# A pre-norm block on one core: the high parts of the probabilities from PSUM, and a new order of issue

## The chip, the cores and the metric

The kernel runs on one core of a Trainium2 chip. The metric is the device time of one execution in microseconds, taken as the median of several runs; the profile shows one further execution with the hardware profiler on.

## The reference

The reference is one transformer block in fp32 over `x` of 4 x 2048 x 256: local attention with 16 heads of 16 elements and a causal window of 64 keys, and then an FFN with ternary weights. Both read a layer norm of their input and are added to it.

```python
q, k, v = proj(h, Wq), proj(h, Wk), proj(h, Wv)          # h = layernorm(x)
scores = einsum('bhqd,bhkd->bhqk', q, k) / 4 + bias       # bias: 0 where i-64 < j <= i, else -inf
x = x + einsum('bsd,ed->bse', softmax(scores) @ v, Wo)
W1q, W2q = quantize(W1), quantize(W2)                     # -1, 0, 1
x = x + relu(layernorm(x) @ W1q.T + b1) @ W2q.T + b2
```

## The kernel before

The 8192 rows are cut into 32 chunks of 256 rows, eight to a sequence. TensorE multiplies in fp16, and every fp32 operand is split into a high part (its rounding to fp16) and a low part (what is left), so that a product is two or three matmuls.

For one chunk the work is this. `load` and `norm_in` fetch the rows, normalize them and transpose them by DMA. `project` makes q, k and v (L635, L627) and their two parts. `stack` copies the parts of q and k by six DMAs (L692) into a buffer `st`, in which one slot per head holds queries, keys, and the keys once more shifted by 64; the shifted copy is made on DVE, the last 64 keys of the chunk before at L705 (at L703 zeros in the first chunk of a sequence) and the rest at L708. `maxima` multiplies queries and keys in 32-row tiles into a PSUM tile `sp` of which there is one (L731), DVE reduces it to the maximum of each row (L738), and four such steps make the maxima of a chunk. ACT scales them (L744), PE transposes them (L750), ACT copies them out (L753), and a DMA on SP's queue writes them as one more row into the stack (L756), so that the following product already has the maximum subtracted.

`weights` then runs eight times for a chunk, for four blocks of 64 queries and two groups of eight heads: eight matmuls of 64 columns (L771) fill one PSUM bank `tp`, ACT takes the exponential into an fp32 tile `pf` in SBUF (L781), ACT casts `pf` to its high part `ph` (L784), and POOL subtracts the two to the low part `pl` (L786). There is a second path with the low part on DVE, which the planner did not take once in this build. `values` multiplies both parts with v (L812 to L814) and divides by the sum (L827, L830). `wo_out` is the output projection (L850 transposes by DMA, L861, L865), the second norm (L573 on ACT with L569 and L570 on POOL, or L577 on DVE; casts and low parts at L579 and L583) and its transposition by DMA (L873). `ffn1` (L896, with L915 on ACT and L917 on DVE, or L906 to L911 with the low part on POOL) and `ffn2` (L936, L937, L942) end the chunk, and L945 stores it.

Six PSUM banks are shared by three kinds of tiles: `lin` (projections and FFN), `tp` (scores) and `pv` (values). A tile's bank is given back by `put`.

The order of the instructions is not that of the source. Each step is a Python generator that yields what it needs next: an engine (`"P"`, `"A"`, `"D"`, `"G"`, `"S"` for PE, ACT, DVE, POOL and SP) with an assumed duration, a buffer, or a signal. `Lanes.run` keeps a clock of its own for each engine and starts, of the steps that could start first, the one with the lowest priority number; the priorities come from the chunk's number and the tables `PRIO`, `SLOPE` and `EARLY` (the last for chunks 0, 1 and 2), less `BOOST` while a step holds a PSUM tile. `Lanes.pick` chooses between ways to do a step by the engines' loads so far, weighted by `WT`. `Lanes.chain` then fixes the order on each engine, SP included, so each engine issues its instructions strictly in the planned order.

```python
cost = [sum(t * math.exp((self.load[e] * WT[e] - top) / TAU) for e, t in o) for o in options]
lanes.add(c * (1 + SLOPE[kind]) + PRIO[kind] + early + 0.001 * k, gen)
```

Of the kernel before, what the change touches and what calls it, by code (L numbers as in the profile page):

```python
# [14 lines left out]
AF = mybir.ActivationFunctionType  # L15
# [4 lines left out]
D = 256  # L20
H = 16
HD = 16
W = 64
FF = 1024
EPS = 1e-5
C = 256
# [4 lines left out]
SW = 16.0  # L31
# [3 lines left out]
NQ = 3  # L35
NV = 3
PARTS = slice(64, 112)
R = 113
BIGH = 60000.0
PRIO = {'norm': 22.87, 'proj': 45.21, 'max': -15.41, 'att': 28.99, 'val': -103.79, 'wo': -72.86, 'ffn': -195.42, 'ffn2': 67.42, 'mask': 69.79, 'prep': -8.89}  # L40
SLOPE = {'norm': 0.0, 'proj': 0.051, 'max': 0.158, 'att': 0.043, 'val': 0.156, 'wo': 0.0, 'ffn': -0.016, 'ffn2': 0.0, 'mask': 0.106, 'prep': -0.017}
BUFS = {'xt': 11, 'ln': 2, 'xT': 3, 'zT': 4, 'qk': 2, 'pp': 6, 'op': 2, 'o': 2, 'h': 7, 'r': 5, 'bank': 6, 'lin': 6, 'sp': 1, 'tp': 3, 'pv': 4}
BANKS = ("lin", "tp", "pv")
EARLY = {'norm': (0.0, 0.0, -1.01), 'proj': (0.0, 6.69, -1.97), 'max': (0.0, 0.0, 0.0), 'att': (0.0, -2.82, 0.0), 'val': (0.0, 6.48, 0.0), 'wo': (0.0, 0.0, -1.66), 'ffn': (0.0, 0.0, 0.0), 'ffn2': (0.69, 0.0, -3.29), 'mask': (0.0, 0.0, 0.0), 'prep': (0.0, -20.19, 0.0)}
TOL = 0.0
BOOST = 4.14
CHAIN = ('PE', 'DVE', 'Activation', 'Pool', 'SP')
LAT = {"P": 0.2, "A": 0.17, "D": 0.15, "G": 0.13, "S": 0.97}
TAU = 17.1
DMAF, DLAT = 1.06, 0.78  # L50
WINDOW = 3.4133
WT = {'P': 0.82, 'A': 1.13, 'D': 1.02, 'G': 0.94, 'S': 0.0}


class Lanes:
# [21 lines left out]
    def put(self, pool):  # L77
        self.slots[pool].append(self.cur[0])
        self.wake(("get", pool))
        if pool == "sp":  # L80
            self.cur[1] += BOOST
        if pool in BANKS:
            self.cur[1] += BOOST
            self.slots["bank"].append(self.cur[0])
            for k in BANKS:
                self.wake(("get", k))
# [9 lines left out]
    def pick(self, options):  # L96

        top = max(self.load[e] * WT[e] for e in "PADG")
        cost = [sum(t * math.exp((self.load[e] * WT[e] - top) / TAU) for e, t in o) for o in options]
        return cost.index(min(cost))  # L100
# [47 lines left out]
    def run(self):  # L148
        while self.ready:
# [29 lines left out]
            if what == "get":  # L179
# [3 lines left out]
                if arg in BANKS or arg == "sp":  # L183
                    task[1] -= BOOST
            elif what == "S":
# [17 lines left out]
def kernel(ctx: ExitStack, tc: tile.TileContext, x, Wq, Wk, Wv, Wo, W1, b1, W2, b2, out):  # L203
    nc = tc.nc
    B, S, _ = x.shape
# [4 lines left out]
    lanes = Lanes(tc, BUFS)  # L210
# [25 lines left out]
    def get(name):  # L236
        return ("get", name)

    def wait(*key):
        return ("wait", key)  # L240

    def signal(*key):
        lanes.signal(key)
# [3 lines left out]
    def start(kind, c, gen, k=0):  # L247
        early = EARLY[kind][int(c)] if c < 3 else 0.0
        lanes.add(c * (1 + SLOPE[kind]) + PRIO[kind] + early + 0.001 * k, gen)

# [8 lines left out]
    st = [const.tile([128, 3, H, C], HP, name=f"st{i}") for i in range(NQ)]  # L259
# [25 lines left out]
    def constants():  # L285
        yield "G", 0.4
        make_identity(nc, ident)
        yield "D", 0.605
        nc.vector.memset(mhalf, -0.5)
        nc.vector.memset(ones, 1.0)  # L290
        nc.vector.memset(shift, PSHIFT * 4.0)
        signal("const")
        yield "D", 0.3
        nc.vector.tensor_copy(identh, ident)
        signal("ident")
        for i in range(NV):
            yield "G", 0.9
            nc.gpsimd.memset(vot[i][:, :, :, :, 32:34], 0.0)
            nc.gpsimd.memset(vot[i][:, 0, :, :, 32:33], 1.0)
            nc.gpsimd.memset(vet[i][0:64, :, 0], 0.0)  # L300
            nc.gpsimd.memset(mht[i % NQ], 0.0)
            signal("vfree", i - NV)
# [36 lines left out]
    def loaded(src, key):  # L339
        yield get("xt")  # L340
        yield "S", (0.5, 0.9)
        wn = xpool.tile([128, 2, D], FP, name="xt")
        nc.sync.dma_start(out=wn, in_=src)
        wts[key] = wn
        signal("loaded", key)
# [162 lines left out]
    def load(c):  # L508
        if c >= 2:
            yield wait("normed", c - 2)  # L510
        yield get("xt")
        yield "S", (0.55, 0.9)
        xt = xpool.tile([128, NT, D], FP, name="xt")
        nc.sync.dma_start(out=xt, in_=xf[c * C:(c + 1) * C, :].rearrange("(t p) d -> p t d", p=128))
        xts[c] = xt
        signal("x", c)
# [159 lines left out]
    def stack(c):  # L676
        first = c % NCB == 0
        yield wait("used", c - NQ)
        s = st[c % NQ]
        if first or (c >= NQ and (c - NQ) % NCB == 0):  # L680

            yield "S", (0.6, 0.1)
            nc.sync.dma_start(
                out=s[R - 1:R, 0], in_=(qone if first else qcon[R - 1:R]).unsqueeze(1).to_broadcast([1, H, C])
            )
            lanes.cur[0] = lanes.free["S"]

        for nm, g, parts in (("q", 0, "hhl"), ("k", 1, "hlh")):
            yield wait(nm, c)
            for n, part in enumerate(parts):  # L690
                yield "S", (0.68, 0.8)
                nc.sync.dma_start(  # L692
                    out=s[64 + n:112:3, g].rearrange("r h t -> r (h t)"),
                    in_=ps_["hl", c][:, g, "hl".index(part)].rearrange("p e t -> p (e t)"),
                )
                if g == 0 or n < 2:
                    lanes.cur[0] = lanes.free["S"]
        ps_.pop(("hl", c))
        put("qk")
        signal("stack", c)  # L700
        yield "D", 0.85
        if first:
            nc.vector.memset(s[PARTS, 2, :, 0:W], 0.0)  # L703
        else:
            nc.vector.tensor_copy(s[PARTS, 2, :, 0:W], st[(c - 1) % NQ][PARTS, 1, :, C - W:])  # L705
            used(c - 1)
        yield "D", 1.4
        nc.vector.tensor_copy(s[PARTS, 2, :, W:], s[PARTS, 1, :, 0:C - W])  # L708
        for b in range(NB):
            start("max", c, maxima(c, b), b)  # L710
            start("val", c, values(c, b), b)

    def place(j):
        return j % 8 * 2 + j // 8

    def window(c, h, b):
        return st[c % NQ][:, 1 if b % 2 else 2, h, b // 2 * 128:b // 2 * 128 + 128]

    def used(c):
        if tally(("used", c), 2 * NB + ((c + 1) % NCB > 0)):  # L720
            signal("used", c)

    def maxima(c, u):
# [35 lines left out]
        for b in range(NB):  # L759
            for g in range(2):  # L760
                start("att", c, weights(c, b, g), 2 * b + g)

    def weights(c, b, g):
        yield get("pp")
        yield get("tp")
        yield "P", 0.24
        tp = tps.tile([128, 8, W], FP, name="bank")
        for i in range(8):
            j = g * 8 + i
            h = place(j)  # L770
            nc.tensor.matmul(tp[:, i], window(c, h, b)[0:R + 1], st[c % NQ][0:R + 1, 0, h, b * W:b * W + W], start=True, stop=True)  # L771
        used(c)
        tpf = tp.rearrange("p h q -> p (h q)")
        ph = pp.tile([128, 4, 128], HP, name="ph")
        pl = pp.tile([128, 4, 128], HP, name="pl")
        phf, plf = (t.rearrange("p a b -> p (a b)") for t in (ph, pl))
        if lanes.pick([[("D", 0.605), ("A", 0.97)], [("G", 1.2), ("A", 1.005)]]):
            yield get("r")
            yield "A", 0.485
            pf = rp.tile([128, 512], FP, name="r")  # L780
            nc.scalar.activation(pf, tpf, AF.Exp, scale=0.25 / (SW * SW))  # L781
            put("tp")
            yield "A", 0.52
            nc.scalar.copy(phf, pf)  # L784
            yield "G", 1.2
            nc.gpsimd.tensor_tensor(plf, pf, phf, ALU.subtract)  # L786
            put("r")
        else:
            yield "A", 0.485
            nc.scalar.activation(tpf, tpf, AF.Exp, scale=0.25 / (SW * SW))  # L790
            yield "A", 0.485
            nc.scalar.copy(phf, tpf)
            yield "D", 0.605
            nc.vector.tensor_tensor(plf, tpf, phf, ALU.subtract)
            put("tp")
        ps_[c, b, g] = (ph, pl)
        signal("p", c, b, g)
# [148 lines left out]
        put("xt")  # L946

    for i, gen in enumerate([constants(), load(0)]):
        lanes.add(-9 + i, gen)
    for i, (nm, src) in enumerate((("q", Wq), ("k", Wk), ("v", Wv))):  # L950
        lanes.add(-7 + i, loaded(src.rearrange("(c p) d -> p c d", p=128), nm))
        start("proj", 0, weight_qkv(nm), i - 5)
    for c in range(NCH):
        if c:
# [34 lines left out]
```

## Time and profile before

| What | us |
|---|---|
| median of 3 runs (lowest, highest) | 670.91 (670.79, 671.71) |
| profiled execution | 671.55 |
| its span, first to last instruction | 669.8 |
| PE busy in the span | 626.2 |
| POOL, DVE, ACT busy | 558.5, 556.4, 529.1 |
| mean granted TensorE clock | 0.987 of full |

Busy time is the union of an engine's instructions; matmuls overlap one another, so a busy PE is not a PE at its peak. A line of a group reads: source line, engine, operation, output and input tiles, shapes, count, busy time in all, mean duration in ns, and the idle time of the engine just before with what ended it. A line of waits reads: who waited, for whom, us in total, how often, the longest. In the tables of stretches each engine has its busy time and, in brackets, its instructions; then come the granted clock, the DMA share and GB/s.

### The profile page before, as it was taken

The numbers are of one execution on the slowest core, as the hardware profiler recorded it, in microseconds if no ns is written. First come the engines' busy times: TensorE is split into PE (matmuls) and PEld (weight loads), VectorE is DVE, ScalarE is ACT, GpSimd is POOL, SyncE is SP. The second block draws the span as 40 slices with busy tenths as digits, with TensorE's granted clock in tenths as the row PEclk, the third lists the DMA queues.
The fourth block names the chain that finished last, engine by engine and source line by source line (L and its number), as shares of the span: only waits on it lengthen the run. The fifth ranks groups of instructions, "written<-read, shape, count | busy, mean of one in ns | idle before, by whom it ended". The sixth has DMA issues, their size and how long they took to land.

```text
span 669.8 us, 30496 instructions
## 1 busy us (share of the span) xinstructions
PE 626.2 (93%) x12892; PEld 548.3 (82%) x12892; DVE 556.4 (83%) x1195; ACT 529.1 (79%) x1074; POOL 558.5 (83%) x639
## 2 busy tenths in 40 slices
PE   2867889999999999999999999999999999999997
PEld 1646777888888888888888879898788888988986
DVE  6788989888987998898989898878878997897763
ACT  6966969877999689988879969686879589987741
POOL 5676989979899879998989979898789689998830
PEclk9977998999999999999999999999999999999999
DMA  6684465766777668865785665589555954542232
GB/s 180 167 154 107 82 130 115 120 129 109 138 132 127 133 115 132 146 115 142 143 140 127 131 96 141 119 142 145 90 124 126 156 122 106 116 107 60 49 81 62
DMA packets 165032, 81.34 MB, mean 121 GB/s; under 512 B 110880, under 2 KB 162848, under 8 KB 164896
## 3 DMA queue, kind: packets, MB, share of 16 engines
q1 hardware_dynamic: 164896, 79.39, 61.5%
q8 instruction: 101, 1.65, 1.2%
q14 instruction: 35, 0.29, 0.2%
HBM read 11.67 MB, written 8.39 MB: 30 GB/s over the span
## 4 chain that ended last, share of the span: by engine, by line
PE 56%; POOL 13%; DVE 11%; ACT 7%; DMA 6%; issue 5%; SPq 3%; POOLq 0%; DVEq 0%; ACTq 0%
PE bank L896 11%; PE bank L635 7%; POOL pl L786 7%; PE bank L771 6%; PE bank L936 6%; PE bank L937 5%; PE sp L731 5%; PE bank L861 5%; PE bank L627 3%; DMA xt<-in_dram 3%; PE bank L814 3%; PE bank L812 2%; PE bank L813 2%; DVE mx L738 2%; ACT ph L784 2%
## 5 line engine op out<-in xcount | busy, mean ns | idle before, releaser
L786 POOL TENSOR_TENSOR pl<-r,ph 128x512 f16<-128x512 f32 x256 | 304.5, 1210 | 17.3 <-ACT ph L784 10.9
L781 ACT ACTIVATE r<-bank 128x512 f32<-128x512 f32 x256 | 145.5, 599 | 32.2 <-PE bank L771 26.9
L784 ACT CAST ph<-r 128x512 f16<-128x512 f32 x256 | 151.0, 629 | 0.7
L738 DVE TENSOR_REDUCE mx<-sp 128x8 f32<-128x768 f32 x128 | 121.8, 952 | 14.7 <-PE sp L731 13.0
L896 PE MATMUL bank<-zT,wq 128*128 128x256 f16 x1024 | 125.5, 273 | 0.3 <-DVE hl L917 0.2
L936 PE MATMUL bank<-wq,hh 128*128 128x256 f16 x512 | 119.7, 273 | 0.0
L937 PE MATMUL bank<-wq,hl 128*128 128x256 f16 x512 | 119.2, 272 | 0.0
L917 DVE SCALAR_TENSOR_TENSOR hl<-bank,hh 128x512 f16<-128x512 f32 x126 | 85.2, 685 | 34.8 <-ACT hh L915 33.2
L896 PEld LDWEIGHTS <-wq 128*128 128x128 f16 x1024 | 97.8, 98 | 12.5 <-issue 0.3
L915 ACT ACTIVATE hh<-bank 128x512 f16<-128x512 f32 x126 | 75.4, 604 | 31.9 <-PE bank L896 31.7
L771 PE MATMUL bank<-st 114*128 114x64 f16 x2048 | 86.9, 194 | 3.8 <-DMA st<-mst 1.4
L812 PEld LDWEIGHTS <-ph 128*128 128x128 f16 x1024 | 82.3, 96 | 4.2 <-DVE o L830 1.8
L814 PEld LDWEIGHTS <-pl 128*128 128x128 f16 x1024 | 79.9, 96 | 5.0 <-POOL pl L786 4.4
L771 PEld LDWEIGHTS <-st 114*128 114x128 f16 x2048 | 74.5, 98 | 11.4 <-issue 2.8
L813 PEld LDWEIGHTS <-ph 128*128 128x128 f16 x1024 | 80.5, 96 | 1.8 <-issue 0.6
L830 DVE TENSOR_TENSOR o<-bank,rec 64x128 f32<-64x128 f32 x256 | 73.8, 288 | 8.4 <-POOL nb L570 0.5
L731 PE MATMUL sp<-st 113*32 113x96 f16 x4096 | 69.7, 211 | 9.5 <-DVE mx L738 4.8
L731 PEld LDWEIGHTS <-st 113*32 113x32 f16 x4096 | 51.3, 98 | 26.9 <-issue 23.9
L936 PEld LDWEIGHTS <-hh 128*128 128x128 f16 x512 | 49.8, 97 | 6.0
L937 PEld LDWEIGHTS <-hl 128*128 128x128 f16 x512 | 50.0, 98 | 4.7
L597 POOL TENSOR_TENSOR op<-o,op 128x512 f16<-128x512 f32 x32 | 39.2, 1225 | 16.6 <-ACT op L844 16.0
L526 DVE BATCH_NORM_STATS2 st<-xt 128x6 f32<-128x256 f32 x128 | 47.8, 415 | 6.0 <-DMA xt<-in_dram 5.0
(117 smaller groups left out, 1493.0 us busy)
## 6 DMA issues: line engine op xcount, KB each, us to landing
st<-hl SPq DMA_DIRECT2D x192, 128.0 KB, 4.1
xt<-in_dram SPq DMA_DIRECT2D x44, 256.0 KB, 4.1
out_dram<-xt SPq DMA_DIRECT2D x32, 256.0 KB, 2.7
ve<-vo SPq DMA_DIRECT2D x32, 136.0 KB, 2.6
ve<-vo SPq DMA_DIRECT2D x60, 68.0 KB, 3.3
oT<-op SPq DMA_TRANSPOSE x64, 3.2
xT<-ht SPq DMA_TRANSPOSE x32, 3.5
st<-mst SPq DMA_DIRECT2D x32, 8.0 KB, 2.2
```

The costliest lines, as they stand in the source:

```text
L731: nc.tensor.matmul(sp[32 * n:32 * n + 32, p, 0:96], st[c % NQ][0:R, 0, h, b * W + q * 32:b * W + q * 32 + 32], window(c, h, b)[0:R, 32 * q ...
L738: nc.vector.tensor_reduce(ps_["mx", c][:, u], sp[:, :, 0:96], AX.X, ALU.max)
L771: nc.tensor.matmul(tp[:, i], window(c, h, b)[0:R + 1], st[c % NQ][0:R + 1, 0, h, b * W:b * W + W], start=True, stop=True)
L781: nc.scalar.activation(pf, tpf, AF.Exp, scale=0.25 / (SW * SW))
L784: nc.scalar.copy(phf, pf)
L786: nc.gpsimd.tensor_tensor(plf, pf, phf, ALU.subtract)
L812: nc.tensor.matmul(pv[:, p, :], ph[:, i, :], v[:, 0, b // 2, p, :], start=True, stop=False)
L813: nc.tensor.matmul(pv[:, p, 0:32], ph[:, i, :], v[:, 1, b // 2, p, 0:32], start=False, stop=False)
L814: nc.tensor.matmul(pv[:, p, :], pl[:, i, :], v[:, 0, b // 2, p, :], start=False, stop=True)
L896: nc.tensor.matmul(ps[:, u], wq1[:, d + d * i, fs], zT[:, i, d], start=n == 0, stop=n == 3)
L936: nc.tensor.matmul(ps[:, t, :], hh[:, f % 2, ts], wq2[:, f, :], start=f == 0, stop=False)
L937: nc.tensor.matmul(ps[:, t, :], hl[:, f % 2, ts], wq2[:, f, :], start=False, stop=f == NF - 1)
```

## The change

There are three edits. In `weights`, on the path that is taken, the high part is no longer cast from `pf` in SBUF: ACT takes the exponential of the same PSUM tile a second time, with fp16 as its output, and the bank is given back after that (`put("tp")` stands one instruction later). In `stack`, the copy of the last 64 keys may go to ACT or DVE by `Lanes.pick`, and the booked durations of the two copies change. The planner's tables change in some entries, so that the order of issue on every engine is another one. `FIRST` is 0 and changes nothing.

```diff
-PRIO = {'norm': 22.87, 'proj': 45.21, 'max': -15.41, 'att': 28.99, ...}
-SLOPE = {'norm': 0.0, ..., 'mask': 0.106, 'prep': -0.017}
+PRIO = {'norm': 22.87, 'proj': 45.21, 'max': -15.28, 'att': 28.41, ...}
+SLOPE = {'norm': 0.051, ..., 'mask': 0.069, 'prep': -0.017}
-EARLY = {..., 'att': (0.0, -2.82, 0.0), 'val': (0.0, 6.48, 0.0), 'wo': (0.0, 0.0, -1.66), ...}
+EARLY = {..., 'att': (4.07, -2.82, 0.0), 'val': (0.0, 6.48, 0.0), 'wo': (0.0, -3.23, -1.66), ...}
-BOOST = 4.14
+FIRST = 0.0
+BOOST = 3.75
-WT = {'P': 0.82, 'A': 1.13, 'D': 1.02, 'G': 0.94, 'S': 0.0}
+WT = {'P': 0.82, 'A': 1.13, 'D': 1.02, 'G': 0.9, 'S': 0.0}
...
-        yield "D", 0.85
         if first:
+            yield "D", 0.85
             nc.vector.memset(s[PARTS, 2, :, 0:W], 0.0)
         else:
-            nc.vector.tensor_copy(s[PARTS, 2, :, 0:W], st[(c - 1) % NQ][PARTS, 1, :, C - W:])
+            old = (s[PARTS, 2, :, 0:W], st[(c - 1) % NQ][PARTS, 1, :, C - W:])
+            if lanes.pick([[("D", 0.7)], [("A", 0.95)]]):
+                yield "A", 0.95
+                nc.scalar.copy(*old)
+            else:
+                yield "D", 0.7
+                nc.vector.tensor_copy(*old)
             used(c - 1)
-        yield "D", 1.4
+        yield "D", 1.5
         nc.vector.tensor_copy(s[PARTS, 2, :, W:], s[PARTS, 1, :, 0:C - W])
...
-        if lanes.pick([[("D", 0.605), ("A", 0.97)], [("G", 1.2), ("A", 1.005)]]):
+        if lanes.pick([[("D", 0.605), ("A", 0.97)], [("G", 1.2), ("A", 0.97)]]):
             yield get("r")
             yield "A", 0.485
             pf = rp.tile([128, 512], FP, name="r")
             nc.scalar.activation(pf, tpf, AF.Exp, scale=0.25 / (SW * SW))
+            yield "A", 0.485
+            nc.scalar.activation(phf, tpf, AF.Exp, scale=0.25 / (SW * SW))
             put("tp")
-            yield "A", 0.52
-            nc.scalar.copy(phf, pf)
             yield "G", 1.2
             nc.gpsimd.tensor_tensor(plf, pf, phf, ALU.subtract)
             put("r")
...
-        lanes.add(-9 + i, gen)
+        lanes.add(FIRST - 9 + i, gen)
```

More of the change, by code (lines that the diff above doesn't have):

```diff
@@ L39 @@
 BIGH = 60000.0
-PRIO = {'norm': 22.87, 'proj': 45.21, 'max': -15.41, 'att': 28.99, 'val': -103.79, 'wo': -72.86, 'ffn': -195.42, 'ffn2': 67.42, 'mask': 69.79, 'prep': -8.89}
-SLOPE = {'norm': 0.0, 'proj': 0.051, 'max': 0.158, 'att': 0.043, 'val': 0.156, 'wo': 0.0, 'ffn': -0.016, 'ffn2': 0.0, 'mask': 0.106, 'prep': -0.017}
+PRIO = {'norm': 22.87, 'proj': 45.21, 'max': -15.28, 'att': 28.41, 'val': -103.79, 'wo': -72.86, 'ffn': -195.42, 'ffn2': 67.42, 'mask': 69.79, 'prep': -8.89}
+SLOPE = {'norm': 0.051, 'proj': 0.051, 'max': 0.158, 'att': 0.043, 'val': 0.156, 'wo': 0.0, 'ffn': -0.016, 'ffn2': 0.0, 'mask': 0.069, 'prep': -0.017}
 BUFS = {'xt': 11, 'ln': 2, 'xT': 3, 'zT': 4, 'qk': 2, 'pp': 6, 'op': 2, 'o': 2, 'h': 7, 'r': 5, 'bank': 6, 'lin': 6, 'sp': 1, 'tp': 3, 'pv': 4}
 BANKS = ("lin", "tp", "pv")
-EARLY = {'norm': (0.0, 0.0, -1.01), 'proj': (0.0, 6.69, -1.97), 'max': (0.0, 0.0, 0.0), 'att': (0.0, -2.82, 0.0), 'val': (0.0, 6.48, 0.0), 'wo': (0.0, 0.0, -1.66), 'ffn': (0.0, 0.0, 0.0), 'ffn2': (0.69, 0.0, -3.29), 'mask': (0.0, 0.0, 0.0), 'prep': (0.0, -20.19, 0.0)}
+EARLY = {'norm': (0.0, 0.0, -1.01), 'proj': (0.0, 6.69, -1.97), 'max': (0.0, 0.0, 0.0), 'att': (4.07, -2.82, 0.0), 'val': (0.0, 6.48, 0.0), 'wo': (0.0, -3.23, -1.66), 'ffn': (0.0, 0.0, 0.0), 'ffn2': (0.69, 0.0, -3.29), 'mask': (0.0, 0.0, 0.0), 'prep': (0.0, -20.19, 0.0)}
 TOL = 0.0
-BOOST = 4.14
+FIRST = 0.0
+BOOST = 3.75
 CHAIN = ('PE', 'DVE', 'Activation', 'Pool', 'SP')
@@ L948 @@
     for i, gen in enumerate([constants(), load(0)]):
-        lanes.add(-9 + i, gen)
+        lanes.add(FIRST - 9 + i, gen)
     for i, (nm, src) in enumerate((("q", Wq), ("k", Wk), ("v", Wv))):
-        lanes.add(-7 + i, loaded(src.rearrange("(c p) d -> p c d", p=128), nm))
+        lanes.add(FIRST - 7 + i, loaded(src.rearrange("(c p) d -> p c d", p=128), nm))
         start("proj", 0, weight_qkv(nm), i - 5)
```

## The prediction

> **What bounds the kernel now.** I read the page's busy shares first, then the chain, then a table of five stretches, because a mean over 670 us hides that the first 66 us are another regime.
>
> ```profile
> PE 626.2 (93%) x12892; PEld 548.3 (82%) x12892; DVE 556.4 (83%) x1195; ACT 529.1 (79%) x1074; POOL 558.5 (83%) x639
> PE 56%; POOL 13%; DVE 11%; ACT 7%; DMA 6%; issue 5%; SPq 3%; POOLq 0%; DVEq 0%; ACTq 0%
> 0.00:66.00 66.00, 39.14 (x531) 29.94 (x532) 50.54 (x114) 48.18 (x102) 42.37 (x63) 0.90 0.68 154
> 66.00:100.00 34.00, 29.00 (x801) 25.64 (x798) 30.01 (x66) 28.25 (x60) 30.58 (x31) 1.00 0.54 102
> 100.00:130.00 30.00, 28.62 (x606) 24.68 (x602) 25.94 (x59) 26.98 (x56) 28.89 (x37) 0.94 0.71 122
> 130.00:660.00 530.00, 523.58 (x10918) 463.07 (x10916) 447.70 (x956) 425.06 (x858) 456.65 (x511) 1.00 0.63 120
> 660.00:670.00 10.00, 5.86 (x54) 5.00 (x52) 2.21 (x4) 0.60 (x1) 0.00 (x0) 1.00 0.15 52
> ```
>
> In the stretches the columns are length, then busy time of PE, weight load, DVE, ACT and POOL, then the granted clock. PE is the bound: from 130 to 660 us it idles 530 - 523.58 = 6.4 us. It idles 26.9 us before 66 us, 5.0 from 66 to 100, 1.4 from 100 to 130 and 4.1 in the last ten. PE does the same matmuls after the change, so its work stays; only idle and slow-clock time can move. In the order of issue, PE's two programs are alike until the transpose of the second chunk's maxima (66 us in this trace), and the last rows are the same final FFN matmuls. So the 26.9 us and the 4.1 us stay, and what can be won is 5.0 + 1.4 + 6.4 = 12.8 us of idle and one slow-clock stretch:
>
> ```profile
> 104.60:108.01 3.41, 2.04 (x83) 1.83 (x79) 3.27 (x11) 3.41 (x8) 3.35 (x5) 1.00 0.44 72
> 108.01:111.42 3.41, 3.41 (x43) 2.63 (x39) 2.57 (x5) 2.44 (x7) 3.33 (x5) 0.50 0.32 60
> ```
>
> Half clock for 3.41 us costs 1.7 us. What PE and the queues wait for (total us, times, longest):
>
> ```profile
> PE sp L731 <- DVE mx L738: 4.8, 7, 1.4
> PE bank L814 <- POOL pl L786: 3.3, 4, 1.2
> PE bank L771 <- DMA st<-mst: 1.4, 1, 1.4
> PE bank L812 <- DVE o L830: 1.4, 1, 1.4
> PE bank L771 <- DVE hl L917: 1.3, 1, 1.3
> POOL pl L786 <- ACT ph L784: 10.9, 8, 3.4
> SPq L850 <- POOL pl L786: 27.4, 13, 4.5
> ```
>
> These are single events, not a pattern.
>
> **The change part by part.** The sum is made against the profiled execution, 671.55 us (span 669.8 and 1.75 around it); the median of the runs, 670.91, lies 0.64 lower.
>
> *Second exponential.* 256 casts from SBUF become 256 exponentials from PSUM.
>
> ```profile
> L786 POOL TENSOR_TENSOR pl<-r,ph 128x512 f16<-128x512 f32 x256 | 304.5, 1210 | 17.3 <-ACT ph L784 10.9
> L781 ACT ACTIVATE r<-bank 128x512 f32<-128x512 f32 x256 | 145.5, 599 | 32.2 <-PE bank L771 26.9
> L784 ACT CAST ph<-r 128x512 f16<-128x512 f32 x256 | 151.0, 629 | 0.7
> L915 ACT ACTIVATE hh<-bank 128x512 f16<-128x512 f32 x126 | 75.4, 604 | 31.9 <-PE bank L896 31.7
> ```
>
> No row is an exponential from PSUM to f16; the nearest are the same exponential to f32 (599 ns) and a relu from PSUM to f16 (604 ns). So ACT saves 256 x (629 - 604) = 6.4 us, at most 256 x (629 - 599) = 7.7. ACT is 79% busy and off the path nearly everywhere: the chain gives L784 2%, 13.4 us, of which 25/629 is 0.5 us. I take -0.5; the ends are 0 and -7.7.
>
> *PSUM bank held longer.* The bank of the scores was free after the first exponential and now is free after the second. In the new order of issue the second stands on average 2.2 ACT instructions behind the first (before, the cast stood 3.8 behind). Three casts take 1.55 us on the chain, so about 0.5 us each: 1.1 us more hold per group. Pairing each of the 256 score groups with its exponential in the trace, the hold now is 1.86 us on average. Six banks serve 22 tiles in each of 32 chunks, 704 in all, so a bank comes round every 6 x 670/704 = 5.7 us: 3.0 us still fits. PE's bank waits today are 1.4 (L812) and 1.3 (L771), with 1.0 more on L771 for DVE's L865: 3.7 us. 1.1 us of 5.7 is a fifth of a bank's round; I take a quarter more waiting, +1.0. The ends are 0 and the second rival's +6.4. The Trainium skill, page "PSUM — Partial Sum Buffer", section "Summary: rules for kernel authors", tells to evacuate PSUM promptly, which speaks against this edit. It gives no price; by it alone the term would be a loss of unknown size, while these rows show a bank's round twice as long as the new hold.
>
> *Low parts and values.* The high part is ready 1.6 ACT instructions, some 0.8 us, earlier. POOL uses little of that: paired in order, its subtraction starts 2.7 us after the cast ends, because POOL is behind. And the new order uses it up: summing PE's start-to-start spacings (0.109 us for 256 columns, 0.025 for L812 to L814, 0.029 for L771, 0.014 for L731) along both orders, the first matmul on a low part stands 8.1 us behind its scores on average, before 9.1. 0.8 won and 1.0 spent: 0, with L814's 3.3 us as the end on both sides.
>
> *Moved loads.* From the order of issue, six instructions of L577 (963 ns) leave DVE, with 6 x 597 ns (L573) on ACT and three pairs of 290 + 195 ns on POOL in their place; two low parts of the FFN go from DVE (685 ns) to POOL (1158 ns). DVE loses 7.1 us, POOL gains 3.8, ACT gains 4.8 (two more casts of 620 included). By the chain's shares (DVE 11%, POOL 13%, ACT 7%) that is -0.8 + 0.5 + 0.3 = 0. If POOL's cover, PE's work, is gone, it is +3.8.
>
> *Copy of the last 64 keys.* All 28 copies stay on DVE (688 ns each) in the built order: the choice is there and never taken. Cost 0; only the planner's booked times differ.
>
> *New order.* In the first stretch that differs, 66 to 130 us, PE idles 6.4 us and loses 1.7 to the clock. By the same spacings the first FFN matmuls (L896), which need none of the attention's engines, come after 58.4 us of PE's work, before 63.0: 4.6 us of filler stands ahead of waits that had none. I take a third of the idle (-2.1) and a bit more than half of the clock's 1.7 (-1.1); the ends are -8.1 and +3.4, a slow stretch twice as long as this one. In the remaining 6.4 us of idle the order is reshuffled with no sign that I can read: 0, from -4 to +4.
>
> The clock's part rests on the row: in the 3.41 us before the slow stretch PE was busy 2.04 us, its longest wait 1.07. The Trainium skill, "TensorE: Matmul & The Clock Gate", section "What's actually happening", has the clock drop after an idle window of some 3.4 us. By that a wait of 1.07 would not slow it and the 1.1 us would not be mine to take (-1.6 in all instead of -2.7); the row shows the drop, so I keep it.
>
> *Sum:* -0.5 + 1.0 + 0 + 0 + 0 - 2.1 - 1.1 = -2.7. 671.55 - 2.7 = 668.85, by the median 668.2.
>
> **Rivals.**
> *The row of maxima queues behind a transpose (slower).* SP issues in order, and the copy of the maxima into the stack (L756) is what every score group of a chunk needs. It stands directly behind a transpose (L850 or L873) in 18 of 32 chunks, before in 8. Transposes wait on SP for POOL, 27.4/13 = 2.1 us each. For: PE's first score group follows its transposed maxima by as little as 4.5 us of work, and ACT's copy (247 ns), the issue (0.57 in the timeline) and the landing (2.2) take 3.0 of them: 1.5 us is left, less than 2.1. Against: the trace has one such wait in 32 chunks (1.4 us; with the weight load's 1.7). If four of the ten new ones run late by 1.6, it is +6.4: 674.6. From two late rows (3.2) the gain is gone. Chance 0.18.
> *Banks run short (slower).* If one score group in twenty (13) finds its bank held for one more ACT instruction, 13 x 0.5 = 6.4: 674.6; it decides from five or six groups. For: the page of waits has bank waits. Against: the 5.7 us round. Chance 0.15.
> *Nothing that shows.* PE's work covers all of it and idle merely moves: 670.9. The profile's 93% speaks for it. Chance 0.17.
> *The stretch is cured.* All 6.4 and 1.7 us go: 670.91 - 0.5 + 1.0 - 8.1 = 663.3. Against: L731 waits for DVE's reduce on its single buffer, which stays. Chance 0.10.
>
> **How the numbers follow.** The forecast, 668.2 (665 to 669.5), has 0.40. Faster by over 0.2% (1.3 us, about what a measurement can tell) is 0.40 + 0.10 = 0.50; within it 0.17; slower 0.18 + 0.15 = 0.33. The range leaves out a part of the cured case below and of the slower cases above: 662.5 to 676.
>
> **What would show it.** Right: the new exponential at about 600 ns; PE's idle from 66 to 130 us near 4 us and no half clock around 108; the first 66 us unchanged to some 0.3 us. Wrong: PE L771 waiting often for ACT's new line (banks) or for the DMA of the maxima (SP), a new half-clock stretch, or PE idle from 130 to 660 above 10 us.

## The result and the profile after

| Kernel | median us (lowest to highest, runs) | profiled execution, span | clock |
|---|---|---|---|
| before | 671.31 (670.79 to 672.28, 4) | 671.55, 669.8 | 0.987 |
| after | 680.85 (679.28 to 682.73, 4) | 679.28, 677.3 | 0.982 |

The ratio is 1.0135 with a 95% interval of 1.0117 to 1.0152: the change makes the kernel slower by some 9 us. The forecast was 668.2, its range ended at 676.0. From L715 on, a line of after is the line of before plus 7 (L771 is L778, L814 is L821); the second exponential stands at L790, and between L44 and L707 it is plus 1.

The page of after, first the busy shares, then the chain, then the groups of the edited path:

```profile
PE 631.2 (93%) x12892; PEld 550.8 (81%) x12892; DVE 557.7 (82%) x1187; ACT 522.6 (77%) x1082; POOL 563.0 (83%) x647
PE 49%; POOL 15%; DVE 11%; ACT 9%; issue 6%; DMA 6%; SPq 2%; POOLq 0%; DVEq 0%; ACTq 0%
...
L793 POOL TENSOR_TENSOR pl<-r,ph 128x512 f16<-128x512 f32 x256 | 307.1, 1220 | 23.4 <-ACT ph L790 11.4
L788 ACT ACTIVATE r<-bank 128x512 f32<-128x512 f32 x256 | 147.5, 612 | 47.0 <-PE bank L778 37.7
L790 ACT ACTIVATE ph<-bank 128x512 f16<-128x512 f32 x256 | 149.9, 620 | 0.0
```

ACT has less to do (522.6 us, before 529.1), and waits longer for PE's scores (37.7 us, before 26.9 on the same line). PE's share of the chain falls from 56% to 49%: the end is set more often by something else. The stretches of after, with the columns of before:

```profile
0.00:66.00 66.00, 39.98 (x543) 30.89 (x544) 51.41 (x119) 49.28 (x104) 42.90 (x64) 0.90 0.68 154
66.00:100.00 34.00, 27.44 (x747) 23.91 (x748) 29.18 (x62) 27.37 (x59) 29.80 (x29) 0.95 0.56 94
100.00:130.00 30.00, 28.07 (x550) 23.91 (x550) 23.86 (x52) 22.51 (x48) 26.75 (x34) 0.89 0.69 128
130.00:660.00 530.00, 522.33 (x10944) 460.32 (x10942) 447.21 (x948) 420.44 (x870) 461.58 (x520) 1.00 0.64 119
660.00:680.00 20.00, 13.41 (x123) 11.77 (x121) 6.00 (x9) 2.98 (x5) 1.99 (x3) 0.94 0.20 57
```

From 66 to 130 us PE is less busy than before, 27.44 + 28.07 us against 29.00 + 28.62, and part of that at half clock; in the long stretch it is 522.33 against 523.58, and the end comes 7.5 us later. PE's own waits, with the first 66 us left out (total us, times, longest):

```profile
PE bank L757 <- DVE o L837: 2.1, 1, 2.1
PE sp L738 <- DVE mx L745: 2.1, 3, 1.2
PE bank L778 <- DVE hl L924: 1.7, 2, 1.4
PE bank L903 <- DVE hl L924: 1.5, 4, 0.6
PE bank L636 <- DVE vo L646: 1.3, 1, 1.3
PE bank L821 <- POOL pl L793: 1.2, 2, 0.8
PE bank L819 <- ACT ph L790: 1.0, 2, 0.6
PE bank L778 <- ACT ph L790: 0.6, 2, 0.4
```

Before, the list began with L814 waiting 3.3 us for POOL's low part. Now six of the eight rows name the last reader of a PSUM bank (L837, L924, L646, L790) and a PE line that takes a bank. No row has PE waiting for the DMA of the maxima.

These rows count only time in which PE stood empty, and matmuls overlap. For a balance that closes I summed, over the matmuls after 66 us, by how much each started later after the one before it than the spacings of the prediction allow; what the granted clock explains was taken off, and the rest put down to the releaser that came last. All traces below are counted so:

| PE waits after 66 us, us | bank | low part | `sp` | DMA | other | sum | lost to the clock |
|---|---|---|---|---|---|---|---|
| before | 6.9 | 5.9 | 3.2 | 1.6 | 0.9 | 18.4 | 1.4 |
| after | 16.1 | 3.1 | 3.2 | 0.4 | 2.7 | 25.5 | 3.8 |

Waits grow by 7.1 and the clock's loss by 2.4, together 9.5; the span grows by 7.5, and PE waits 1.1 less in the first 66 us (31.6 for 32.7; 32.6 in a repeat, so no effect of the change). That leaves 0.9 us that the balance does not place. By kind the growth is in bank waits, +9.2, against -2.8 for low parts. By place the waits go from 8.4 to 11.5 us in the stretch from 66 to 130, from 2.8 to 6.6 up to 300, from 5.8 to 3.8 up to 500 and from 1.5 to 3.5 behind: the loss is spread out, and no single wait holds it.

### The profile page after: what moved, and what is told of

Its sections match the earlier page's. It is cut to its first block, busy times and chain, and to the rows that moved or that the text cites. A ratio compares the mean times of both kernels' runs of the same rounds, so it can differ in the third digit from the quotient of the medians.

```text
span 677.3 us, 30547 instructions
## 1 busy us (share of the span) xinstructions
PE 631.2 (93%) x12892; PEld 550.8 (81%) x12892; DVE 557.7 (82%) x1187; ACT 522.6 (77%) x1082; POOL 563.0 (83%) x647
## 4 chain that ended last, share of the span: by engine, by line
PE 49%; POOL 15%; DVE 11%; ACT 9%; issue 6%; DMA 6%; SPq 2%; POOLq 0%; DVEq 0%; ACTq 0%
PE bank L903 10%; POOL pl L793 7%; PE bank L636 6%; PE sp L738 5%; PE bank L943 5%; PE bank L778 5%; PE bank L944 5%; PE bank L868 5%; PE bank L628 3%; DMA st<-hl 3%; PE bank L821 2%; PE bank L819 2%; PE bank L820 2%; ACT ph L790 2%; DMA xt<-in_dram 2%
## 5 line engine op out<-in xcount | busy, mean ns | idle before, releaser
L788 ACT ACTIVATE r<-bank 128x512 f32<-128x512 f32 x256 | 147.5, 612 | 47.0 <-PE bank L778 37.7
L790 ACT ACTIVATE ph<-bank 128x512 f16<-128x512 f32 x256 | 149.9, 620 | 0.0
L903 PE MATMUL bank<-zT,wq 128*128 128x256 f16 x1024 | 125.8, 273 | 2.0 <-DVE hl L924 1.5
L924 DVE SCALAR_TENSOR_TENSOR hl<-bank,hh 128x512 f16<-128x512 f32 x124 | 84.2, 686 | 36.5 <-ACT hh L922 35.2
L903 PEld LDWEIGHTS <-wq 128*128 128x128 f16 x1024 | 97.9, 98 | 15.5 <-issue 2.2
L778 PE MATMUL bank<-st 114*128 114x64 f16 x2048 | 86.5, 194 | 3.0 <-DVE hl L924 1.7
L819 PEld LDWEIGHTS <-ph 128*128 128x128 f16 x1024 | 82.4, 96 | 2.4
L778 PEld LDWEIGHTS <-st 114*128 114x128 f16 x2048 | 75.6, 98 | 10.2 <-issue 3.8
L821 PEld LDWEIGHTS <-pl 128*128 128x128 f16 x1024 | 79.8, 96 | 2.5 <-POOL pl L793 2.0
L837 DVE TENSOR_TENSOR o<-bank,rec 64x128 f32<-64x128 f32 x256 | 74.0, 289 | 8.1
L738 PEld LDWEIGHTS <-st 113*32 113x32 f16 x4096 | 51.4, 98 | 26.2 <-issue 23.3
L532 POOL TENSOR_TENSOR rs<-rs,mhalf 128x2 f32<-128x2 f32 x64 | 45.9, 718 | 5.3
```

The source lines that it names most:

```text
L738: nc.tensor.matmul(sp[32 * n:32 * n + 32, p, 0:96], st[c % NQ][0:R, 0, h, b * W + q * 32:b * W + q * 32 + 32], window(c, h, b)[0:R, 32 * q ...
L790: nc.scalar.activation(phf, tpf, AF.Exp, scale=0.25 / (SW * SW))
L819: nc.tensor.matmul(pv[:, p, :], ph[:, i, :], v[:, 0, b // 2, p, :], start=True, stop=False)
L821: nc.tensor.matmul(pv[:, p, :], pl[:, i, :], v[:, 0, b // 2, p, :], start=False, stop=True)
L903: nc.tensor.matmul(ps[:, u], wq1[:, d + d * i, fs], zT[:, i, d], start=n == 0, stop=n == 3)
```

## The experiments

All kernels here compute the whole reference. Each was timed beside the kernel before.

### Undoing the edits by halves

Three kernels split the change, and a fourth takes one table back.

The order of after on every engine, with only the operation put back:

```diff
-            nc.scalar.activation(phf, tpf, AF.Exp, scale=0.25 / (SW * SW))
+            nc.scalar.copy(phf, pf)
```

> The changed kernel's order of issue, instruction for instruction on every engine, but the high part is again a cast from the fp32 tile in SBUF, so that the bank of the scores is free after the first exponential. Theory 'order' (the loss comes with the new order of issue, first of all as idle time and half-clock stretches of PE between 66 and 150 us): the time stays at that of the changed kernel, 679 to 682 us, with three half-clock stretches between 80 and 125 us as there. Theory 'bank' (PE waits for banks that the second exponential holds): most of the 9.5 us come back, 671 to 674 us, and PE's waits for the exponential's line go. If the exponential from PSUM is a gain by itself, this one is slower than the changed kernel by up to 2 us.

Measured: 683.33 us (682.2 to 684.82), ratio 1.0168 [1.0136, 1.0200]. Repeated later beside after itself:

> The changed kernel's order with the cast from SBUF once more, beside the changed kernel itself. Theory 'any new plan': within 3 us of it, above rather than below, since the cast is the slower operation and the bank's earlier return buys little. Theory 'scarce banks' in its first form: 6 us or more below it.

> The changed kernel once more, beside the next one on the same chip: 679 to 683 us.

Measured: with the cast 682.2 us, 1.0156 [1.0134, 1.0178]; after 680.73 us, 1.0127 [1.0102, 1.0151]. The page of the first run with the cast, two groups, and behind them PE's waits after 66 us:

```profile
L788 ACT ACTIVATE r<-bank 128x512 f32<-128x512 f32 x256 | 145.4, 599 | 43.6 <-PE bank L778 36.7
L790 ACT CAST ph<-r 128x512 f16<-128x512 f32 x256 | 152.6, 624 | 0.7
```

```profile
PE sp L738 <- DVE mx L745: 3.9, 6, 1.2
PE sp L738 <- DVE st L715: 2.9, 5, 0.9
PE bank L821 <- POOL pl L793: 2.6, 5, 1.0
PE bank L778 <- DVE o L837: 1.6, 2, 1.2
PE bank L903 <- DVE hl L924: 1.4, 3, 0.6
```

So in the new order the edit of the operation costs nothing: after, with the second exponential, is 1.5 us faster than with the cast where both ran together, with intervals that overlap. Both times lie just above the 679 to 682 us of the theory 'order' and far from the 671 to 674 of the theory 'bank'. The bank is free early again (from a group's first score matmul to its release 2.04 us on average, 3.02 in after) and bank waits fall to 11.6 and 11.0 us in the two runs, but PE then waits for `sp`, for keys (DVE's copies at L715) and for low parts instead: 26.6 and 27.2 us in all, after 25.5 and 27.4. The 9 us belong to the order. That the held bank causes the bank waits of after is true of each row and false of the total.

The change with the old tables (`PRIO`, `SLOPE`, `EARLY`, `BOOST`, `WT` of before in the code of after), and the old code with the new tables:

> The changed code (second exponential, choice of the copy's engine, its booked times) with the planner's tables of before; the planner makes an order of its own from them. Theory 'order': what counts is the plan, so this may land anywhere between 670 and 685 us, and where it lands goes with the idle time of PE and the half-clock stretches before 150 us. Theory 'bank': slow like the changed kernel, 678 to 683 us, with waits for the exponential's line all along the span.

> The code of before (cast from SBUF, bank given back after the first exponential, the planner knows that) with the tables of the changed kernel. Theory 'order', if the tables themselves are to blame: 677 to 683 us, with a loss before 150 us. Theory 'bank': 670 to 674 us.

Measured: 685.12 us, 1.0197 [1.0169, 1.0226], and 681.9 us, 1.0144 [1.0114, 1.0173]. Each half alone costs as much as both, or more; for the second the theory 'order' had 677 to 683 us, 'bank' 670 to 674. The new tables do better with the new code than the old ones do (680.85 against 685.12), as tables that were fitted to the later release would, but not back to 671; that they were fitted so is not shown. With one table of them taken back:

```diff
-EARLY = {..., 'att': (4.07, -2.82, 0.0), 'val': (0.0, 6.48, 0.0), 'wo': (0.0, -3.23, -1.66), ...}
+EARLY = {..., 'att': (0.0, -2.82, 0.0), 'val': (0.0, 6.48, 0.0), 'wo': (0.0, 0.0, -1.66), ...}
```

> The changed kernel with one table, EARLY, as before (scores of chunk 0 not put off by 4.07, output projection of chunk 1 not drawn ahead by 3.23). Theory 'order', with the loss made by these two entries in the first chunks: PE idles less and runs at full clock more between 66 and 150 us, 673 to 677 us. If the two entries are not the cause: 679 us or more, or a plan of its own with its own losses. Theory 'bank': 678 to 683 us.

Measured: 690.63 us, 1.0280 [1.0242, 1.0318]. Two entries of a table for the first chunks are worth 10 us of the whole in this plan, and against the expectation that they make the loss: without them it is twice as large.

### The held bank at the old order

The prediction's bank term needs the order kept. All 256 second exponentials can't stand in before's order, for a bank would be wanted before it is given back. But where the cast stands no more than five ACT instructions behind its exponential, it can be one: 208 of 256. Every instruction keeps its place on its engine. (`NEAR` is 5; `lanes.nact`, kept in lines that are not shown, counts the instructions that ACT was given so far.)

```diff
             put("tp")
+            at = lanes.nact
             yield "A", 0.52
-            nc.scalar.copy(phf, pf)
+            if lanes.nact - at <= NEAR:
+                nc.scalar.activation(phf, tpf, AF.Exp, scale=0.25 / (SW * SW))
+            else:
+                nc.scalar.copy(phf, pf)
```

> The order of before, instruction for instruction on every engine, with one operation exchanged: 208 of the 256 casts, those that stand at most five ACT instructions behind their exponential, are the second exponential from PSUM (for the other 48 the bank would be held across work that waits for it). Tables, booked times and the planner's idea of the bank are those of before. Theory 'any new plan' (the operation is harmless, the new order costs the time): 669 to 673 us, ACT's busy time some 4 us less. Theory 'scarce banks' in its first form (the longer hold itself makes PE wait): 675 us or more, with PE's waits for banks up from 6.9 us towards 16.

Measured: 685.1 us (683.35 to 687.48, 5 runs), 1.0201 [1.0175, 1.0227]. Its groups, and PE's waits after 66 us (here L784 is the first exponential, L789 the second, L774 the scores):

```profile
L784 ACT ACTIVATE r<-bank 128x512 f32<-128x512 f32 x256 | 146.2, 602 | 44.0 <-PE bank L774 37.0
L789 ACT ACTIVATE ph<-bank 128x512 f16<-128x512 f32 x208 | 118.8, 612 | 0.0
```

```profile
PE bank L819 <- ACT ph L789: 2.5, 3, 1.0
PE bank L821 <- POOL pl L793: 1.5, 2, 1.1
PE bank L774 <- ACT ph L789: 1.4, 3, 0.9
...
PE bank L868 <- ACT ph L789: 1.3, 2, 0.9
...
PE bank L903 <- ACT ph L789: 1.1, 2, 0.7
...
PE bank L753 <- ACT ph L789: 0.7, 1, 0.7
PE bank L630 <- ACT ph L789: 0.7, 1, 0.7
```

This is the clean case. The operation is no dearer than the cast (612 ns against 629), the order is the same, and only the release is later: 2.94 us of hold on average, before 1.86. Bank waits go from 6.9 to 22.9 us and all waits from 18.4 to 31.8; with 2.4 more lost to the clock that is 15.8, and the span grew by 15.9. The releaser in those rows is the new line, and the waiters are all the lines that take a bank: values (L819), scores (L774), output projection (L868), FFN (L903), transposed maxima (L753), v (L630). The values' matmuls (L819) also read `ph`, but in all three of their waits the exponential named belongs to a score group one to three behind those that they read, so they too wait for a bank. And from each tile's first matmul to the end of its last reader, all six banks are held at once for 63.9 us of before and for 129.0 us here (after 122.5, and 65.8 in after's order with the cast). So at before's order the late release costs 13 to 14 us: the theory 'scarce banks' holds, and 'any new plan', which had 669 to 673 us here, does not cover it.

The planner told of the late release, in before with the cast kept and booked at the exponential's 0.485, makes yet another order:

```diff
-            put("tp")
-            yield "A", 0.52
+            yield "A", 0.485
             nc.scalar.copy(phf, pf)
+            put("tp")
```

> The kernel before, tables and all, with one edit: the planner is told that the bank of the scores comes free after the cast instead of after the first exponential (and the cast is booked at 0.485 instead of 0.52); the cast itself still reads SBUF. The planner makes a new order from it. Theory 'scarce banks' (planning with the longer hold packs the other bank users so tightly that PE waits for banks whenever DVE or ACT run late): 679 to 686 us, PE's waits for banks after 66 us at 10 us or more, against 6.9 in the kernel before and 16.1 in the changed one. Theory 'any new plan' (the order of before is an unusually good one, and whatever makes the planner start over costs about 10 us): 679 to 686 us too, but then the two small edits of this batch cost as much. Theory 'tables' (the new tables are to blame): 670 to 674 us.

Measured: 690.27 us, 1.0263 [1.0243, 1.0283]. That is above every range that was expected. Its bank waits are 7.5 us, not the 10 or more of 'scarce banks': the plan does avoid them, and pays with 8.3 on DMAs, 5.1 on keys and 8.3 on the clock.

### Is it this order, or any other than the old one?

Three kernels keep the instructions that the code of before asks for and change one thing that only the planner sees: the booked times of `stack`'s copies (0.85 to 0.7 for the last 64 keys, 1.4 to 1.5), two entries of `PRIO` (`max` -15.41 to -15.28, `att` 28.99 to 28.41), or one of `WT` (`G` 0.94 to 0.9). The work is the same, but `Lanes.pick` decided anew too, so the expectations' words on unchanged instructions hold only nearly: one low part of the FFN in the first kernel and two in the others went from POOL to DVE, and two instructions of the norm (L577) in the second and four in the third from DVE to ACT.

> The kernel before with only the booked times of the two copies into the stack changed as in the change (0.7 for 0.85, 1.5 for 1.4); no instruction is added, removed or replaced, but the planner's order differs from the second quarter of the span's first tenth on. Theory 'any new plan': 677 to 686 us. Theories 'scarce banks' and 'tables': 670 to 674 us.

> The kernel before with only two priorities changed as in the change (max -15.28 for -15.41, att 28.41 for 28.99): the same instructions in another order. Theory 'any new plan': 677 to 686 us, with PE's waits after 66 us at 25 us or more, against 18.4 before. Theory 'scarce banks': 670 to 674 us. Theory 'tables': between 672 and 681, as these two are part of them.

> The kernel before with only the weight of POOL's load changed as in the change (0.90 for 0.94). PE's order is the same for the first 58% of its instructions and differs after that. Theory 'any new plan': the second half alone loses, 673 to 678 us, all of it after 390 us. Theories 'scarce banks' and 'tables': 670 to 674 us.

| | median us | ratio [95%] | bank | DMA | all waits | clock |
|---|---|---|---|---|---|---|
| booked times | 680.99 | 1.0137 [1.0107, 1.0166] | 11.7 | 3.1 | 26.2 | 3.0 |
| `PRIO` | 681.2 | 1.0130 [1.0110, 1.0150] | 17.0 | 0.3 | 27.6 | 1.3 |
| `WT` | 681.97 | 1.0133 [1.0111, 1.0156] | 7.3 | 8.4 | 25.6 | 4.2 |

Each costs what the whole change costs, and each by other waits. That is the range of 'any new plan' (677 to 686 us), and above its 673 to 678 for `WT`; 'scarce banks' and 'tables' had 670 to 674 for the first and the last. `PRIO` loses to banks with the early release still in force. `WT` has PE's order of before for its first 58% and loses at the very end. Its waits of PE, one row, and its last stretches:

```profile
PE bank L896 <- DMA zT<-ht: 6.2, 1, 6.2
```

```profile
655.00:660.00 5.00, 5.00 (x47) 4.31 (x44) 3.03 (x7) 0.64 (x2) 1.36 (x4) 1.00 0.00 0
660.00:665.00 5.00, 0.08 (x1) 0.00 (x0) 0.69 (x1) 1.71 (x3) 2.49 (x4) 0.99 0.27 76
665.00:670.00 5.00, 3.71 (x18) 2.66 (x19) 0.69 (x1) 0.68 (x2) 0.00 (x0) 0.50 0.17 32
```

The last chunk's FFN needs its norm and a transposing DMA, and PE has only what is left of chunks 29 and 30 to do meanwhile. In before 12.2 us of such work stand there and PE doesn't wait; here only 3.5, and PE stands still for 6.2 us and then runs at half clock. If that is the whole loss, holding back work for that gap mends it:

```diff
-        early = EARLY[kind][int(c)] if c < 3 else 0.0
+        early = (EARLY[kind][int(c)] if c < 3 else 0.0) + (300.0 if kind in ('ffn','ffn2') and 29 <= c < 31 else 0.0)
```

> The kernel that was before with POOL's weight at 0.90, and one more edit: the FFN steps of chunks 29 and 30 get 300 added to their priority number, so that they are held back and stand between the last chunk's output projection and its FFN. By PE's spacings 10.5 us of other matmuls stand there, against 3.5 without the edit and 12.2 in the kernel before; PE's order is the same up to the last two per cent. Theory 'the tail is a cliff' (what that kernel lost is PE waiting for the transposed second norm of the last chunk, 6.4 us, and the half clock that follows, 2.7): 672 to 675 us. If the loss lies elsewhere: it stays at 680 to 682 us.

Measured: 671.9 us (671.05 to 673.84, 10 runs), 1.0003 [0.9989, 1.0016]: all of it is back, with 10.5 us of work in the gap and 18.6 us of waits in all. It equals the kernel before and doesn't beat it. The choices of engine are those of `WT`, so these cost nothing. The same gap stands in three more of the plans: 3.5 us of work and 6.2 of waiting with the late release booked, 7.0 and 2.8 with the booked times, 7.4 and 2.6 with the old `EARLY`. Work and wait make 9.7 to 10.1 us each time, and the plans with 10.5 us or more wait 0.3 at most. After has 11.8 us there and loses nothing at its end, so this repair is not one for it.

## Why the prediction was wrong

**The bank term (+1.0, ends 0 and +6.4) was mis-sized.** At the order for which it was worked out it is +13 to +14, beyond its upper end. The mechanism, 1.1 us more hold, was right to a tenth (1.86 to 2.94 and 3.02). What failed is "a bank comes round every 6 x 670/704 = 5.7 us: 3.0 us still fits". The tiles are not alike. Measured from a tile's first matmul to its last reader in the trace of before, an FFN output (L936) holds its bank 16.4 us, a tile of q or k 8.3, one of v 6.9, scores and values about 2, and a hidden tile of the FFN (L896) 3.0. The 3.0 us that were to fit are the scores' hold alone; all 704 holds make 2522 us, 3.6 each and 63% of six banks' 669.8 us, and after 2756, 68%. A count of tiles says nothing of how often long holds fall together: all six banks were taken for 63.9 us of before already, and the later release doubles that. Then one more microsecond is on PE's path. The bank's last reader stood in 3.7 us of the rows of before; that was read as small and raised by a quarter, where bank waits went from 6.9 to 22.9 us. The Trainium skill, "PSUM — Partial Sum Buffer", section "Summary: rules for kernel authors", with its advice to evacuate promptly, was put aside for the 5.7 us round; the kernel with only the release moved sides with the page.

**The new order (-3.2, and 0 from -4 to +4 for the rest) was the step that decided.** It was taken as neutral outside the first stretch, since no sign could be read. In the order of after the operation makes no difference beyond 1.5 us, and the order itself costs 10 to 11. Three orders that no edit of an instruction asked for cost about 9 as well. So the order of before is a much better one than the neighbours tried, and leaving it was a loss to be expected, not a coin to be tossed around zero: PE idled 6.4 us of 530 there, which leaves little to win and much to lose. The two losses do not add up: the release costs 13 to 14 at the old order and nothing more in the new one, and the new order costs 10 to 11 by itself. "A third of the idle is won" from 66 to 130 us came out as 8.4 us of waits before and 11.5 after; the 4.6 us of FFN filler did not help.

**The half clock (-1.1).** Forecast to be cured, it became three stretches in place of one between 66 and 130 us, here the last two with the 3.4 us ahead of each:

```profile
96.70:100.10 3.40, 1.76 (x75) 1.45 (x75) 3.06 (x5) 3.40 (x9) 3.40 (x3) 1.00 0.63 96
100.10:103.51 3.41, 3.41 (x56) 2.52 (x45) 2.28 (x4) 1.03 (x3) 3.35 (x5) 0.50 0.71 140
113.70:117.10 3.40, 1.87 (x48) 1.60 (x45) 3.25 (x6) 3.18 (x9) 3.40 (x4) 1.00 0.50 97
117.10:120.50 3.40, 3.40 (x39) 2.65 (x38) 2.20 (x6) 3.06 (x7) 3.40 (x3) 0.51 0.44 111
```

But the price of 1.7 us for each is doubtful too. The repeat of after has none of the three:

```profile
66.00:130.00 64.00, 55.89 (x1398) 49.48 (x1395) 55.56 (x128) 53.96 (x115) 60.02 (x67) 1.00 0.64 112
```

Set matmul against matmul, the repeat is 0.9 us behind at 80 us, 3.4 ahead at 130, and only 2.0 ahead at 200, 0.8 at 350 and 0.5 at the end: spans 676.8 and 677.3, medians 680.73 and 680.85. It loses 3.8 us less to the clock and waits 1.9 more. So of 4.3 us that the full clock won by 130 us, 2.9 went back into waits, some of them on DMAs (1.7 us, in after 0.4). This is one pair of executions; it shows that a half-clock stretch is not a term to be added up at its full price, not what one is worth.

**What held.** The copy of the last 64 keys stayed on DVE, but not at its 688 ns: it took 862 in after and 792 in the repeat, 4.9 and 2.9 us more of DVE that the sum has at 0; what they cost PE is not shown. The first 66 us moved little, if more than the 0.3 us allowed (PE busy 39.98 and 39.62 us, before 39.14). PE's end was not touched, though in other orders the end is where much goes. (The 4.1 us of idle that the prediction reads in the last ten count 0.2 us behind the program's end at 669.8.) Low parts: the forecast of 0 with 3.3 either way met -2.8. ACT was off the path, as said: 9 us less of ACT (522.6 against 531.7 with the cast in the same order) brought the kernel 1.5. But the saving is not to be read where the sum read it. The second exponential took 620 ns, not 599 to 604, and the first went from 599 to 612, so that the two groups' own time is that of before (147.5 + 149.9 = 297.4, before 145.5 + 151.0 = 296.5). Instructions on ACT overlap in the trace, and the saving shows from start to start (last section).

**The rivals.** "Banks run short" had the right mechanism and 0.15; its price of 6.4 was half of the 13 to 14 at the old order. "The row of maxima queues behind a transpose" did not happen: PE's waits on DMAs went from 1.6 to 0.4 us (1.7 in the repeat), and none of after's rows has PE wait for the maxima. No rival had a new order that is worse for no reason in the edit, and the range, at 676.0, ended 1.4 us above what either slower rival came to alone (674.6).

**What stays open.** Which property makes the old order good is not settled: bank waits in one neighbour, the end of the program in another, `sp`, keys and banks in the new order with the cast. Three small steps off it are few, and each cost about the same by different waits; an order that beats both kernels was not found. The time with all six banks held is not the one property either: 91.9 us with the booked times and 108.9 with `PRIO`, but 65.8 in after's order with the cast and 58.5 with `WT`, before 63.9. The cause of the bank waits that the new order keeps with the early release (11 us, before 6.9) was not tried.

## What to carry to other kernels

When a planner writes the order, an edit is judged only with the order held fixed (is the new wait there?) and with the operation undone in the new order (is the old time back?); the two can have different answers, as here. If PE is 98 to 99% busy in the long stretch, take a re-plan as a likely loss of the size that small changes of the planner's numbers make, and measure two or three of these first. For buffers that unlike tiles share, add up holds by kind and look at the longest, and at how long all buffers are held at once, not at the mean time between uses.

## What the runs showed of the hardware

Half clock began after 3.4 us in which PE was busy 1.76 us and its longest wait was 1.2 us, and in the repeat of the same kernel it did not begin at all between 66 and 130 us. Yet there, too, PE is busy only 1.17 us of the 3.41 us from 78.99 us on, at a granted clock of 1.00. What differs, as far as the traces show, is where such a stretch lies. In each of the fourteen traces the half-clock stretches begin whole multiples of 3.413 us apart (in after at 83.0, 100.1 and 117.1 us), so each run has a grid of windows of this length, which lies elsewhere in the next run. Between 66 and 640 us, every window of these grids that ran at full clock with less than 1.7 us of busy PE was followed by half clock (7 of 7); with 1.76 to 2.48 us it went both ways. The repeat's idle stretch falls on two windows with 2.14 and 2.44 us of busy PE. The Trainium skill, "TensorE: Matmul & The Clock Gate", section "What's actually happening", speaks of an idle window and of one that runs free of the kernel; the second agrees with these grids and with two runs of one program that differ, the first only loosely, since PE was half busy in these windows.

The exponential of a 128x512 PSUM tile to fp16 took 612 to 620 ns, about the cast of the same size from SBUF (624 to 629). ACT's total is shorter by more than these means show: 522.6 us against 531.7 with the cast in the same order, where the four durations add up to 297.4 and 298.0. From start to start the two differ more. Where ACT does not idle, the next instruction starts 477 ns (median) after the second exponential in after, and 508 to 520 ns after the cast. For some 230 of the 256 that is 31 to 43 ns each, 7 to 10 us. And in the 21 cases where the second step stands directly behind its own exponential, which the cast reads and the second exponential doesn't, the two take 1.11 us together instead of 1.25.

The copy of the last 64 keys (48x1024 in fp16, DVE) takes 417 to 434 ns in 11 of its 28 executions in before. 16 others begin while POOL is in an addition or subtraction of 128x512 (L786, L583, L597, L882), and every one of them ends 282 to 288 ns after the end of that instruction, up to 1332 ns after its own start. In after 20 do. So a copy's time hangs on what POOL is doing, and the mean rises to 862 ns.
